# Windowed attention by halves of the rows, beside a mixture of experts: moving the first half's output groups among the second half's rounds

## The chip, the core and the metric

The kernel runs on one core of a Trainium2 chip. The core has five engines with instruction queues of their own: TensorE (PE) multiplies matrices, VectorE (DVE) does elementwise work and reductions, ScalarE (ACT) evaluates functions, GpSimd (POOL) does slower elementwise work and issues indirect DMAs, and SyncE (SP) issues DMAs. Each engine works through its queue in order and waits on semaphores for the others. The metric is the device time of one execution in microseconds (us); a run is repeated and its median is given.

## What is computed

One transformer block on x of shape 2 x 1024 x 256. The rows are normalized; windowed attention and a routed mixture of experts both read the normalized rows, and their results are added to x:

```
xn = layernorm(x)
x  = x + attn(xn) + ffn(xn)
# attn: tok = xn as tokens of 16 values; q, k, v = tok @ qkv_w
#   per branch (8 of the 16 channels): windows of 8 tokens, along a line or down a column
#   out = softmax(q * scale @ k^T) @ v + conv3x3(v) + bias
#   att = concat(out1, out2) @ proj_w + proj_b
#   tok + (att - mean) * rsqrt(var + eps) * ln_w + ln_b, transposed back to rows
# ffn: scores = sigmoid(xn @ gate^T); 6 of 16 experts a row, from 2 of 4 groups
#   out = sum over experts of weight * (silu(xn @ g^T) * (xn @ u^T)) @ d^T
#   + a shared expert of twice the width
```

All values are 32-bit floats.

## The kernel before

After the layer norm, the routing and the shared expert (the first 110 us or so), the kernel is one loop over 55 units of routed expert work with two half units each (the loop over `u` at L1098). A unit is either "six" (two of the six most wanted experts of one of 16 sorted tiles of 128 rows, `xsT`) or "extra" (two lists of 128 rows that have another expert, gathered by an indirect DMA, `gathered`, L978, and turned on TensorE, `turned`, L984). For one half unit TensorE multiplies rows by the expert's two input matrices into `pr_u` (`up`, L849), ScalarE takes Silu into `sg`, and VectorE multiplies `sg`, the row's weight and the second product into `hms` (L856). A unit later TensorE transposes `hms` into `ph` (`hidden`, L863), ScalarE copies it to `hT`, and another unit later the down product goes into `pr_y` (L879, L887), is copied to `ysum` and is added to the output in memory by an indirect DMA from GpSimd's queue (`to_out`, L992, its DMA at L994). All writes that add to the output go one after another, since each waits for the landing of the one before.

Attention is done beside this loop. It is written as a list of small steps, a generator `walk` (`attention_steps`, L1052), each with an estimated cost on VectorE and on TensorE. After each half unit the loop takes steps as long as VectorE's sum of costs is not ahead of `pace` times TensorE's (L1120). `pace` is made so that the walk is done when `END` = 72 us of TensorE's work is still left (L1074 to L1078). The order in which instructions stand in each engine's queue then comes from a scheduler in the framework, which may move an instruction ahead of others that are not ready in its reckoning.

The walk has four rounds, `attention(b, h)` for two images b and two halves h of a row's 256 values (h is 128 columns). A round (L653 to L745) gathers its input from the transposed rows `xnT`, projects it on TensorE in eight matmuls `pq` whose results ScalarE copies to `qk` and `v`, and then works on VectorE: four products `pr` and four reductions `s` (scores), a maximum, the subtraction, Exp on ScalarE, four products `pv` and four reductions `o`, a division into `xo`. TensorE turns `xo` (`po`, L725) and ScalarE copies it into `oT` (L727), one tile of 4 groups x 2 halves x 4 x 128 columns. The rounds go b by b: (0,0), (0,1), (1,0), (1,1).

After the fourth round come eight output groups, `attended(g, h, ...)` for g = 0 to 3 and both halves (L761): four matmuls of 512 columns into `pp` (three for the convolution, from `xnT`, one for the projection of `oT`; the first and the last group read a shifted copy of the edge rows, `xe`, made by `edges`, L747), a bias on ScalarE into `a` (L780), four transposes `pa`, Square (L787), a sum on VectorE (`var`, L789), Sqrt on ScalarE (L790), a reciprocal (L791), a product (L792), and on GpSimd a multiplication by `lw` (L793) and two additions of the normalized row `xr` into `att` (L798). `xr` is loaded for each g by a DMA from GpSimd's queue (L769). After g = 1 and g = 3, four DMAs of 256 KB each add `att` to the output (`attention_added`, L1065, L1068). The working tiles `a`, `sq` and `xr` use the three buffers `f1024` that the rounds had, so no group can start before the last round is over. ScalarE has one table of functions loaded at a time: Sqrt, Exp and Silu are in different ones, and a change shows as ACT_TABLE_LOAD.

While the loop runs, the lists of the extra units are made (`lists_begun`, L900) in `room_`, a part of `ysum`, until half unit 45.

Of the kernel before, what the change touches and what calls it, by code (L numbers as in the profile page):

```python
# [8 lines left out]
F32 = mybir.dt.float32  # L9
# [3 lines left out]
AF = mybir.ActivationFunctionType  # L13
# [9 lines left out]
P = 128  # L23
B, H, W = 2, 1024, 256
# [27 lines left out]
def csw_block_moe(ctx: ExitStack, tc: tile.TileContext, x, qkv_w, conv_w0, conv_b0, conv_w1, conv_b1,  # L52
# [33 lines left out]
    def by_hl(t):  # L86
        return t.rearrange("(p l) d -> p l d", l=16)
# [659 lines left out]
    def edges():  # L747

        xe = [work.tile([P, 2, 4, P], F32, tag=tag, name="xe") for tag in ("v", "xo")]
        for t in xe:
            nc.gpsimd.memset(t, 0.0)
        pairs = xnT.rearrange("p h l (q e) -> p l h q e", e=2)
        for h in range(2):
            above, below = (t[:, h].rearrange("p l (q e) -> p l q e", e=2) for t in xe)
            nc.vector.tensor_copy(above[:, :, :, 1], pairs[:, 12:16, h, :, 0])
            nc.vector.tensor_copy(below[:, :, :, 0], pairs[:, 0:4, h, :, 1])
        return xe

    def attended(g, h, xe, att):  # L761

        if not last_room:
            last_room.extend(work.tile([P, 2, TB], F32, tag="f1024", name=name, bufs=3) for name in ("xr", "a", "sq"))
        xr = last_room[0].rearrange("p l (k d) -> p (l k) d", d=W)
        quarters = [t[:, n] for t in last_room[1:] for n in range(2)]
        a_, sq_ = quarters[(2 * g + h) % 3], quarters[3]
        if h == 0:
            nc.gpsimd.dma_start(out=xr, in_=by_hl(xw_d[0:ROWS, :])[:, 4 * g : 4 * g + 4, 0:W])  # L769
# [3 lines left out]
                 (lp[:, 1], xnT[:, h, 4 * g - 4 : 4 * g, :] if g > 0 else xe[0][:, h]),  # L773
                 (lp[:, 2], xnT[:, h, 4 * g + 4 : 4 * g + 8, :] if g < 3 else xe[1][:, h]),
# [4 lines left out]
        aT = a_.rearrange("p (l q) -> p l q", l=4)  # L779
        nc.scalar.activation(aT, pp, AF.Identity, bias=pbc)  # L780
# [5 lines left out]
        sq, a = (t.rearrange("p (n c) -> p n c", c=C) for t in (sq_, a_))  # L786
# [6 lines left out]
        nc.gpsimd.tensor_tensor(a, a, lw.unsqueeze(1).to_broadcast(wide), ALU.mult)  # L793
        for m in range(2):
            to = att[m].rearrange("p n (l d) -> p n l d", d=16)[:, :, 4 * g : 4 * g + 4, 8 * h : 8 * h + 8]
            one = a.rearrange("p (l t) c -> p c l t", t=8)[:, 8 * m : 8 * m + 8]
            two = xr.rearrange("p l (t c) -> p c l t", c=C)[:, 8 * m : 8 * m + 8, :, 8 * h : 8 * h + 8]
            nc.gpsimd.tensor_tensor(to, one, two, ALU.add)  # L798

    last_room = []  # L800
# [97 lines left out]
    listed = []  # L898

    def lists_begun():  # L900
# [47 lines left out]
        lists_ended()  # L948
        yield
# [102 lines left out]
    def attention_steps():  # L1052
        for b in range(B):
            for h in range(2):
                yield from attention(b, h)
        xe = []
        yield 0.6, 0.0, lambda: xe.extend(edges())
        att.extend(work.tile([P, 8, W], F32, tag=tag, name="att") for tag in ("prod", "qk"))
        for g in range(4):
            for h in range(2):  # L1060
                yield 1.4, 3.9, lambda: attended(g, h, xe, att)
            if g % 2:
                waiting.extend([lambda m=m, b=b, n=g // 2: attention_added(m, b, n) for m in range(2) for b in range(B)])

# [9 lines left out]
    END = 72  # L1074
    in_walk = [8 * 1.0 + 4 * (16 * 2.3 + 3.3 + 2.5 + 1.5 + 1.4) + 0.6 + 8 * 1.4, 8 * 0.1 + 4 * 6.2 + 8 * 3.9]
# [22 lines left out]
    for u in range(len(laid_out) + 2):  # L1098
        for q in range(2):
# [20 lines left out]
            while step and done[0] <= pace * done[1]:  # L1120
# [82 lines left out]
```

## Time and profile before

| | |
|---|---|
| runs | 447.02, 447.40, 449.18 us, median 447.4 |
| profiled execution | 447.97 us, span from first to last instruction 446.3 us |
| busy: PE, DVE, ACT, POOL | 393.4, 291.5, 214.1, 197.9 us |
| mean granted TensorE clock | 0.987 |
| four rounds of attention, on VectorE | 4 x 4 of each of pr, s, pv, o at 2.27 to 2.29 us |
| output groups on TensorE | 347.5 to 397.7 us from the start of the span |

Durations and positions are those of one profiled execution. The busy time of an engine is that in which an instruction of it runs; "waited for" is idle time before an instruction with the instruction that ended it. Matmuls overlap, and the profile shows each as longer than its share of a dense sequence, so I take TensorE's costs from the chain that ended last, where successive pieces don't overlap. In the loop, a half unit's product pr_u takes TensorE 1.28 us.

### The profile page before, as it was taken

What the parts mean: (1) busy time and instruction counts of PE and PEld (TensorE: products, weight loads), DVE (VectorE), ACT (ScalarE), POOL (GpSimd) and SP (SyncE); (2) the same over time, 40 slices, a digit from 0 to 9 for tenths busy, and PEclk for the clock granted to TensorE, in tenths of its full rate; (3) what the DMA queues carried; (4) which work ended last, traced back from release to release, by engine and by line L of the source; (5) the groups of instructions that cost most, each with busy time, mean ns of one, the idle gap of its engine ahead of it and who ended that gap; (6) DMA issues with size and microseconds to landing.
All of it is one profiled execution on the core that took longest, in us unless ns stands there. A gap on an engine that the chain in (4) does not pass through costs nothing.

```text
span 446.3 us, 6293 instructions
## 1 busy us (share of the span) xinstructions
PE 393.4 (88%) x1668; PEld 246.3 (55%) x1669; DVE 291.5 (65%) x515; ACT 214.1 (48%) x535; POOL 197.9 (44%) x207
## 2 busy tenths in 40 slices
PE   0999999997899788998897999999998899979990
PEld 0435465664466555565564666656665555446670
DVE  4624958635699979289995999959999223322210
ACT  2945258322544442643635456364533657774320
POOL 7300000314273299457524245615554274779432
PEclk9999999999999999999999999999999999998997
DMA  8999941324023101101212124210332101822922
GB/s 232 338 304 321 275 154 30 64 67 86 25 71 73 32 25 34 29 23 33 38 39 60 35 43 81 47 36 24 69 90 56 22 14 57 103 68 74 126 44 24
DMA packets 40178, 37.56 MB, mean 84 GB/s; under 512 B 5300, under 2 KB 37616, under 8 KB 40112
## 3 DMA queue, kind: packets, MB, share of 16 engines
q0 software_dynamic: 11616, 13.52, 18.4%
q1 hardware_dynamic: 27472, 22.59, 16.4%
q10 hardware_dynamic: 1056, 1.05, 0.7%
q8 instruction: 15, 0.25, 0.2%
q14 instruction: 19, 0.16, 0.1%
HBM read 27.70 MB, written 12.45 MB: 90 GB/s over the span
## 4 chain that ended last, share of the span: by engine, by line
DVE 38%; PE 30%; DMA 10%; issue 8%; ACT 7%; POOL 5%; DVEq 0%; POOLq 0%; ACTq 0%; SPq 0%
DVE s L688 6%; PE pr_u L853 6%; DVE pv L705 6%; DVE pr L684 5%; DVE o L710 5%; DVE hms L856 5%; PE pp L777 4%; PE pq L671 3%; PE pr_y L879 3%; DMA out_dram<-ysum,lists 3%; PE pg L273 3%; PE py L288 2%; DMA xg<-xw_d,lists 2%; PE pu L273 2%; DMA xx<-in_x_dram 2%
## 5 line engine op out<-in xcount | busy, mean ns | idle before, releaser
L853 PE MATMUL pr_u<-w1s,xsT 128*128 x384 | 128.4, 468 | 3.4 <-DVE hms L856 2.4
L853 PEld LDWEIGHTS pr_u<-w1s,xsT 128*128 128x128 f32 x384 | 69.9, 191 | 39.4 <-issue 7.7
L994 POOL DMA_INDIRECT out_dram<-ysum,lists x30 | 57.2, 1908 | 77.4 <-ACT ysum L1040 20.3
L855 ACT ACTIVATE sg<-pr_u 128x176 f32<-128x176 f32 x110 | 34.7, 317 | 77.1 <-PE pr_u L853 70.2
L856 DVE SCALAR_TENSOR_TENSOR hms<-sg,w,pr_u 128x176 f32<-128x176 f32 x96 | 36.8, 387 | 35.5 <-ACT sg L855 35.5
L684 DVE TENSOR_TENSOR pr<-qk 128x2048 f32<-128x2048 f32 x16 | 36.6, 2288 | 17.6 <-ACT qk L673 17.2
L705 DVE TENSOR_TENSOR pv<-s,v 128x2048 f32<-128x2048 f32 x16 | 36.5, 2284 | 2.5 <-ACT s L696 2.4
L867 PE MATMUL ph<-ident,hms 128*128 128x128 f32 x165 | 31.7, 282 | 5.5 <-DVE hms L856 2.9
L688 DVE TENSOR_REDUCE s<-pr 128x256 f32<-128x2048 f32 x16 | 36.5, 2279 | 0.1
L955 POOL TENSOR_SCALAR ysum<-row_h,spot 128x128 f16<-128x128 f16 x26 | 28.0, 1094 | 19.2 <-PE rows_of L946 14.9
L710 DVE TENSOR_REDUCE o<-pv 128x256 f32<-128x2048 f32 x16 | 36.3, 2269 | 0.0
L980 POOL DMA_INDIRECT xg<-xw_d,lists x14 | 21.6, 1540 | 29.3 <-DVE hms L856 15.5
L867 PEld LDWEIGHTS ph<-ident,hms 128*128 128x128 f32 x165 | 21.5, 144 | 23.2 <-DVE hms L856 6.9
L291 POOL DMA_DIRECT2D out_dram<-ysh x4 | 3.7, 928 | 64.5 <-ACT ysh L289 64.5
L817 POOL DMA_INDIRECT xg<-xw_d,lists x16 | 19.8, 1239 | 25.4 <-PE ph L867 9.3
L879 PE MATMUL pr_y<-w2a,hT 128*128 x96 | 29.1, 386 | 0.0
L879 PE MATMUL pr_y<-wts,hT 128*128 128x256 f32 x96 | 29.0, 384 | 0.0
L879 PE MATMUL pr_y<-w2b,hT 112*128 x96 | 28.8, 381 | 0.0
L671 PE MATMUL pq<-wq,rows 128*128 128x384 f32 x64 | 25.1, 506 | 3.3 <-ACT oT L727 1.9
L869 ACT COPY hT<-ph 128x384 f32<-128x384 f32 x55 | 26.4, 480 | 2.8 <-PE ph L867 1.8
L853 PE MATMUL pr_u<-w1s,xd 128*128 x56 | 20.4, 487 | 6.6 <-ACT xd L989 6.6
L288 PE MATMUL py<-room 128*128 128x256 f32 x96 | 23.9, 387 | 0.7 <-DVE room L282 0.7
(403 smaller groups left out, 712.2 us busy)
## 6 DMA issues: line engine op xcount, KB each, us to landing
w1s<-in_w_dram SPq DMA_DIRECT2D x22, 256.0 KB, 4.4
wts<-in_w_dram SPq DMA_DIRECT2D x55, 64.0 KB, 2.1
wts<-in_w_dram SPq DMA_DIRECT2D x55, 48.0 KB, 1.7
xw_d<-xx SPq DMA_DIRECT2D x4, 544.0 KB, 4.6
w2a<-in_w_dram SPq DMA_DIRECT2D x4, 512.0 KB, 9.4
out_dram<-ysh POOLq DMA_DIRECT2D x4, 512.0 KB, 5.6
xr<-xw_d POOLq DMA_DIRECT2D x4, 512.0 KB, 5.0
out_dram<-att POOLq DMA_DIRECT2D x8, 256.0 KB, 6.4
```

What stands on the lines that cost most here:

```text
L288: nc.tensor.matmul(py, lhsT=hms[k, m][:, P * c : P * c + P], rhs=w2h[:, m], start=(m == 0), stop=(m == 2))
L671: nc.tensor.matmul(pq.rearrange("p s t c -> p (s t c)"), lhsT=rows[:, i], rhs=wq.rearrange("p s t c -> p (s t c)"), start=True, stop=True)
L684: nc.vector.tensor_tensor(pr, q_.unsqueeze(3).to_broadcast(full), k_.unsqueeze(2).to_broadcast(full), ALU.mult)
L688: nc.vector.tensor_reduce(out=s[:, n : n + NW], in_=held.pop(n), axis=AX.X, op=ALU.add)
L705: nc.vector.tensor_tensor(pr, s[:, n : n + NW].unsqueeze(3).to_broadcast(full), v[:, br, m : m + NW].unsqueeze(2).to_broadcast(full), ALU. ...
L710: nc.vector.tensor_reduce(out=o[:, n : n + NW], in_=held.pop(n), axis=AX.X, op=ALU.add)
L853: nc.tensor.matmul(pu, lhsT=lhs[:, h, :], rhs=w1s[:, :, h, bass.ds(e * I, I)], start=(h == 0), stop=(h == 1))
L855: nc.scalar.activation(sg, pu[:, 0, :], AF.Silu)
L856: nc.vector.scalar_tensor_tensor(hm[:, 0:I], sg, w, pu[:, 1, :], op0=ALU.mult, op1=ALU.mult)
L867: nc.tensor.transpose(ph[:, s, :], units[:, P * s : P * s + P], ident)
L879: nc.tensor.matmul(py, lhsT=l_, rhs=r_, start=start and n == 0, stop=stop and n == 2)
L994: nc.gpsimd.indirect_dma_start(out=out_rows, out_offset=bass.IndirectOffsetOnAxis(ap=index, axis=0), in_=ys, in_offset=None, bounds_check= ...
```

## The change

The rounds are ordered by half: (0,0), (1,0), (0,1), (1,1). After two rounds `oT` is complete for half 0, so its output groups can start. `attended` is cut into two steps: `attended` (the four matmuls and the bias) and `normed` (the transposes, the norm and the multiplication by `lw`). The eight steps of half 0 are put among the rounds of half 1, one ahead of every fourth step of a round from its second VectorE step on. The bias result and the normalized values are written back into `oT`, in the place of the group's input, so no working tile is needed but one for the squares; this and the edge rows lie in `room_`, and a step of 3 us or more of TensorE work waits until the lists are made (`made`). The edge copy is made for one half and one edge at a time, four times, in one tile. The additions of `xr` (`added`) stay behind the last round for both halves, since `att` uses the rounds' buffers; the loads of `xr` for three groups are issued together there, the fourth behind the additions of group 0. `END` goes from 72 to 50, and the cost of the steps is counted anew.

```diff
--- before.py
+++ after.py
@@ -744,46 +744,41 @@
             steps.append((0.3, 0.5, lambda i=i: transposed(i)))
         return steps
-    def edges():
-        xe = [work.tile([P, 2, 4, P], F32, tag=tag, name="xe") for tag in ("v", "xo")]
-        for t in xe:
-            nc.gpsimd.memset(t, 0.0)
-        pairs = xnT.rearrange("p h l (q e) -> p l h q e", e=2)
-        for h in range(2):
-            above, below = (t[:, h].rearrange("p l (q e) -> p l q e", e=2) for t in xe)
-            nc.vector.tensor_copy(above[:, :, :, 1], pairs[:, 12:16, h, :, 0])
-            nc.vector.tensor_copy(below[:, :, :, 0], pairs[:, 0:4, h, :, 1])
-        return xe
-    def attended(g, h, xe, att):
-        if not last_room:
-            last_room.extend(work.tile([P, 2, TB], F32, tag="f1024", name=name, bufs=3) for name in ("xr", "a", "sq"))
-        xr = last_room[0].rearrange("p l (k d) -> p (l k) d", d=W)
-        quarters = [t[:, n] for t in last_room[1:] for n in range(2)]
-        a_, sq_ = quarters[(2 * g + h) % 3], quarters[3]
-        if h == 0:
-            nc.gpsimd.dma_start(out=xr, in_=by_hl(xw_d[0:ROWS, :])[:, 4 * g : 4 * g + 4, 0:W])
+    def edge(h, n):
+        t = room_[:, TB : 2 * TB].rearrange("p (l q) -> p l q", l=4)
+        nc.gpsimd.memset(t, 0.0)
+        pairs = xnT[:, h].rearrange("p l (q e) -> p l q e", e=2)
+        nc.vector.tensor_copy(t.rearrange("p l (q e) -> p l q e", e=2)[:, :, :, 1 - n],
+                              pairs[:, 0:4, :, 1] if n else pairs[:, 12:16, :, 0])
+        return t
+    def attended(g, h):
+        xe = edge(h, g // 3) if g % 3 == 0 else None
         pp = ps_m.tile([P, 4, P], F32, tag="m", name="pp")
         terms = [(lp[:, 0], xnT[:, h, 4 * g : 4 * g + 4, :]),
-                 (lp[:, 1], xnT[:, h, 4 * g - 4 : 4 * g, :] if g > 0 else xe[0][:, h]),
-                 (lp[:, 2], xnT[:, h, 4 * g + 4 : 4 * g + 8, :] if g < 3 else xe[1][:, h]),
+                 (lp[:, 1], xnT[:, h, 4 * g - 4 : 4 * g, :] if g > 0 else xe),
+                 (lp[:, 2], xnT[:, h, 4 * g + 4 : 4 * g + 8, :] if g < 3 else xe),
                  (wp, oT[:, g, h])]
         for n, (l_, r_) in enumerate(terms):
             nc.tensor.matmul(pp.rearrange("p l q -> p (l q)"), lhsT=l_.rearrange("p t c -> p (t c)"),
                              rhs=r_.rearrange("p l q -> p (l q)"), start=(n == 0), stop=(n == len(terms) - 1))
-        aT = a_.rearrange("p (l q) -> p l q", l=4)
-        nc.scalar.activation(aT, pp, AF.Identity, bias=pbc)
+        nc.scalar.activation(oT[:, g, h], pp, AF.Identity, bias=pbc)
+    def normed(g, h):
+        aT = oT[:, g, h]
         pa = ps_m.tile([P, 4, P], F32, tag="m", name="pa")
         for l in range(4):
             nc.tensor.transpose(pa[:, l, :], aT[:, l, :], ident)
         rows_a = pa.rearrange("p l (t c) -> p (l t) c", c=C)
         wide = [P, 32, C]
-        sq, a = (t.rearrange("p (n c) -> p n c", c=C) for t in (sq_, a_))
+        sq, a = room_[:, 0:TB].rearrange("p (n c) -> p n c", c=C), aT.rearrange("p l (t c) -> p (l t) c", c=C)
         nc.scalar.activation(sq, rows_a, AF.Square)
         var = small.tile([P, 32], F32, tag="var", name="var")
         nc.vector.tensor_reduce(out=var, in_=sq, axis=AX.X, op=ALU.add)
@@ -791,13 +786,19 @@
         nc.vector.reciprocal(var, var)
         nc.vector.tensor_tensor(a, rows_a, var.unsqueeze(2).to_broadcast(wide), ALU.mult)
         nc.gpsimd.tensor_tensor(a, a, lw.unsqueeze(1).to_broadcast(wide), ALU.mult)
+    def rows_of_x(g):
+        xr = work.tile([P, 2, TB], F32, tag="f1024", name="xr", bufs=3).rearrange("p l (k d) -> p (l k) d", d=W)
+        nc.gpsimd.dma_start(out=xr, in_=by_hl(xw_d[0:ROWS, :])[:, 4 * g : 4 * g + 4, 0:W])
+        return xr
+    def added(g, h, xr, att):
+        a = oT[:, g, h].rearrange("p l (t c) -> p (l t) c", c=C)
         for m in range(2):
             to = att[m].rearrange("p n (l d) -> p n l d", d=16)[:, :, 4 * g : 4 * g + 4, 8 * h : 8 * h + 8]
             one = a.rearrange("p (l t) c -> p c l t", t=8)[:, 8 * m : 8 * m + 8]
             two = xr.rearrange("p l (t c) -> p c l t", c=C)[:, 8 * m : 8 * m + 8, :, 8 * h : 8 * h + 8]
             nc.gpsimd.tensor_tensor(to, one, two, ALU.add)
-    last_room = []
     xsT = big.tile([P, NTL, 2, P], F32, name="xsT", tag="xx")
@@ -895,7 +896,7 @@
     at_ = room_[:, 0 : 3 * 257].rearrange("p (a n) -> p a n", a=3)
     begin = room_[:, 800:832].rearrange("p (a e) -> p a e", a=2)
     ends = route.tile([P, E], F32, name="ends")
-    listed = []
+    listed, made = [], []
     def lists_begun():
         flagged = room_[:, 832:960].bitcast(BF16)
@@ -946,6 +947,7 @@
                 nc.tensor.matmul(listed[0], lhsT=spot[:, 0:P], rhs=spot[:, P:], start=(n == 2), stop=(n == NX + 1))
             yield
         lists_ended()
+        made.append(True)
         yield
     def pair_listed(n):
@@ -1050,17 +1052,29 @@
         yield from attention_steps()
     def attention_steps():
-        for b in range(B):
-            for h in range(2):
-                yield from attention(b, h)
-        xe = []
-        yield 0.6, 0.0, lambda: xe.extend(edges())
+        ahead_ = [step for g in range(4) for step in of_group(g, 0)]
+        for h in range(2):
+            for b in range(B):
+                for n, step in enumerate(attention(b, h)):
+                    if h == 1 and n >= 10 and n % 4 == 2 and ahead_:
+                        yield ahead_.pop(0)
+                    yield step
+        yield from ahead_
+        xr = [rows_of_x(g) for g in range(3)]
         att.extend(work.tile([P, 8, W], F32, tag=tag, name="att") for tag in ("prod", "qk"))
         for g in range(4):
-            for h in range(2):
-                yield 1.4, 3.9, lambda: attended(g, h, xe, att)
+            yield 0.0, 0.0, lambda: added(g, 0, xr[g], att)
+            yield from of_group(g, 1)
+            yield 0.0, 0.0, lambda: added(g, 1, xr[g], att)
+            if g == 0:
+                yield 0.0, 0.0, lambda: xr.append(rows_of_x(3))
             if g % 2:
                 waiting.extend([lambda m=m, b=b, n=g // 2: attention_added(m, b, n) for m in range(2) for b in range(B)])
+    def of_group(g, h):
+        yield 0.2, 3.45, lambda: attended(g, h)
+        yield 1.4, 0.45, lambda: normed(g, h)
     def attention_added(m, b, n):
@@ -1071,8 +1085,8 @@
     of_slot = {"six": (0.5, 2.0), "extra": (0.8, 2.5)}
     of_tile = (0.75, 0.25)
-    END = 72
-    in_walk = [8 * 1.0 + 4 * (16 * 2.3 + 3.3 + 2.5 + 1.5 + 1.4) + 0.6 + 8 * 1.4, 8 * 0.1 + 4 * 6.2 + 8 * 3.9]
+    END = 50
+    in_walk = [8 * 1.0 + 4 * (16 * 2.3 + 3.3 + 2.5 + 1.5 + 1.4) + 8 * 1.6, 8 * 0.1 + 4 * 6.2 + 8 * 3.9]
     done = [0.0, 0.0]
     whole = [in_walk[n] + NTL * TOPK * of_slot["six"][n] + NL * of_slot["extra"][n] + NTL * of_tile[n] for n in range(2)]
     pace = (whole[0] - END * of_slot["six"][0] / of_slot["six"][1]) / (whole[1] - END)
@@ -1117,7 +1131,7 @@
                 if 0 <= u - 2 < len(laid_out):
                     finished(laid_out[u - 2], hT_.pop(u - 2), wts[:, (u - 2) % 3], begun_.pop(u - 2))
             counted(of_slot[laid_out[min(u, len(laid_out) - 1)][0]])
-            while step and done[0] <= pace * done[1]:
+            while step and done[0] <= pace * done[1] and (made or step[1] < 3):
                 step[2]()
                 counted(step)
                 last, step = step, next(walk, None)
```

## The prediction

> **What bounds the kernel now.** I read the shares by engine first (TensorE 88% busy, VectorE 65%), then busy time by stretch, since a mean hides stages. The stretches are the three last attention rounds (from the first product to the last division) and the stretch of the eight output groups.
>
> ```profile
> core 0: us, PE busy (x) PEld busy (x) DVE busy (x) ACT busy (x) POOL busy (x), PEclk, DMA share, GB/s
> ...
> 188.00:238.50 50.50, 45.26 (x193) 30.02 (x191) 48.10 (x47) 21.61 (x68) 26.86 (x28) 1.00 0.16 36
> ...
> 244.30:292.00 47.70, 45.30 (x188) 30.26 (x186) 46.71 (x41) 22.83 (x65) 22.15 (x12) 1.00 0.27 53
> ...
> 298.00:346.00 48.00, 44.65 (x188) 29.54 (x187) 46.98 (x43) 20.91 (x63) 23.15 (x13) 1.00 0.26 56
> 346.00:400.00 54.00, 50.55 (x180) 27.56 (x177) 16.43 (x33) 37.26 (x55) 32.07 (x29) 1.00 0.31 53
> ```
>
> Columns are stretch, length, then PE, PE loads, DVE, ACT, POOL busy. In the rounds VectorE is busy 141.8 of 146.2 us (97%): it is the limit, and TensorE (135.2 of 146.2) follows it. In the last row it is the reverse: VectorE 16.4 of 54, TensorE 50.6 of 54. So 16 us of dense TensorE work stands where VectorE is free, beside rounds where VectorE is full. What TensorE waits for from 188 to 346 us (total, times, longest):
>
> ```profile
> PE pr_u L853 <- ACT xd L989: 4.1, 10, 0.5
> PE po L725 <- DVE xo L718: 3.2, 3, 1.6
> PE ph L867 <- DVE hms L856: 2.0, 5, 0.6
> PE pq L671 <- ACT oT L727: 1.2, 2, 0.7
> PE ph L867 <- ACT hT L869: 1.1, 1, 1.1
> ```
>
> 6.3 us (po for xo, ph for hms and hT) are lateness of VectorE and of the activations behind it. The other 5.9 (xd, oT, a gather of 0.6) are single round trips that no order removes. Then the chain that ended last, at the start of the output groups:
>
> ```profile
> 345.68 0.67 PE po L725 x4
> ...
> 347.48 3.71 PE pp L777 x8
> 351.22 0.70 ACT a L780
> 351.96 0.66 PE pa L783 x4
> ...
> 355.01 3.45 PE pp L777 x8
> ```
>
> The first group starts at 347.5, when the last round's oT is there. One costs TensorE 3.45 us (pp, eight passes) and 0.67 (pa). Last the GpSimd queue to the end:
>
> ```profile
> 381.22 4.82 POOL L1068 DMA_DIRECT2D out_dram<-att  x4
> ...
> 392.52 1.67 POOL L994 DMA_INDIRECT out_dram<-ysum,lists  x1 [4.37 <-DMA out_dram<-att]
> ...
> 411.38 4.77 POOL L1068 DMA_DIRECT2D out_dram<-att  x4
> 421.95 1.66 POOL L994 DMA_INDIRECT out_dram<-ysum,lists  x1 [5.80 <-DMA out_dram<-att]
> ...
> 439.04 1.55 POOL L994 DMA_INDIRECT out_dram<-ysum,lists  x1 [3.06 <-DMA out_dram<-ysum,lists]
> ```
>
> The end is not TensorE's: its last matmul is over at 435.9. After the second block of four att stores (411.38) come five scatters, each waiting for the landing before it (10.6 us for the stores, then 17.1 from first to last scatter), and 7.3 us more to 446.3. From that block to the end is 34.9 us, and it is a chain of GpSimd and DMA.
>
> **The change part by part.** Sums are made against the profiled execution: span 446.3, time 447.97, so 1.67 lies around it; the median of the runs, 447.4, is 0.6 lower, which I take off at the end.
>
> *Order.* The order of the built program shows that the four groups of half 0 now stand among the two rounds of half 1, one at each of the half units 53, 61, 70 and 75 of 114, and that the last group stands just before the last pair of extra units, as before. The wait for finished lists (made) holds nothing: they are done at half unit 45. The rounds end 4 half units later (91, not 87).
>
> *Moved TensorE work.* Ahead of the last stretch now lie 4 groups of 3.45 + 0.67 = 16.5 us and 4 half units of experts: 4 x 1.28 (pr_u) + 2 x (0.33 + 1.30) (ph, pr_y) + 0.6 (px) + 0.8 (waits for xd) = 9.8. The start of the last stretch moves from 347.5 to 373.8. TensorE's sum is unchanged: this alone is worth nothing.
>
> *Relief of VectorE.* From 188 to 346 it worked 142.7 of 158 us (90%, gaps between the rounds counted). It gets four norms (var 0.69, reciprocal 0.35, product 0.69: 6.9), edge copies (0.6) and 4 more hms (0.39 each: 1.6), 151.8 in all, over 158 + 26.3: 82%. Inside the rounds, whose three gaps of 5.3 us for projections stay, it is 152 of 168 or 90% instead of 97%. Of the 6.3 us of lateness I take half, -3.2 (ends 0 and -6.3): a hms must still stand behind a 2.29 us product, but no more behind several. The rounds of half 0 are paced 7% slower (pace falls from 1.18 to 1.10); of 4.7 us of such waits from 117 to 188 I take -1.0 (0 to -2). Groups 0 to 3 now have half units of experts between pp and pa, where pa waited 2.3 us for a in 346 to 400: half of it, -1.2.
>
> *Activations in the rounds.* A norm brings sq 0.60, a table load, sqrt 0.32, and a load back to Silu:
>
> ```profile
> 353.53 1.28 ACT L790 ACT_TABLE_LOAD   x1
> 354.82 0.32 ACT L790 ACTIVATE var<-var,eps 128x32 f32<-128x32 f32 x1
> 355.16 1.28 ACT L855 ACT_TABLE_LOAD   x1
> ```
>
> Loads in total fall from 30 to 29; four pairs move into the rounds, in front of sg and hT. The Trainium skill (ScalarE: Activation LUTs, "What ACT_TABLE_LOAD costs") gives a switch of set 1283 ns and a drain of 1380, 2.66 us together. The row has the 1283, and sqrt starts 0.01 us after its load ends: no drain lies between. By the page a norm would hold ScalarE 5.3 us in loads, by the row 2.6. The nearest row for what TensorE loses is the Exp of the three rounds, also two loads around one activation: at 214 ph waits 1.15 + 0.31, at 267 nothing, at 323 0.31. Mean 0.6, so four norms cost +2.4 (0 to +6; by the page about double). Below nothing is excluded, since no load is taken away here.
>
> *GpSimd in the rounds.* Multiplying by lw (1.27 us alone) now runs beside 2.29 us products that read two SBUF operands. The Trainium skill (SBUF, State Buffer, "Who interferes with whom") speaks against that: such an instruction and a GpSimd instruction that reads SBUF shut each other out, whichever starts first. The trace has GpSimd's side: a spots comparison takes 0.59 alone and 2.62 at 161.70, beside pv (161.55 to 163.85). By the rule VectorE could lose 1.27 x 4 = 5.1 as well; in the rows pv takes 2.30 where GpSimd began 0.3 earlier and 2.28 elsewhere. I take 0 for VectorE, and up to 2.3 x 4 on GpSimd, which is idle half of the rounds (26.9 of 50.5 busy); without that cover the queue's gathers would be 2 us late, where the one issued at 251.86 has its px at 262.19, 10 us later. The four memsets replace two of twice the size; each is issued when the edge before it has been read, far ahead of its group, so pp doesn't wait for them: 0 (up to +1).
>
> *The last stretch.* From its start T the groups of half 1 take 4 x (3.45 + 1.28 + 0.67) + 2 x 1.65 = 24.9 us. GpSimd: its six additions of half 0 whose xr is there (1.05 each) and three xr issues are over by about T+1; memset to T+2.5; then the first lw product waits for group 0's norm until T+9.3 (as at 356.48, 9.0 after pp), additions to T+12.7, the fourth xr is issued behind them and lands 4.3 us later, additions of group 3 to T+19.6, lw and additions of group 1 to T+23. First block of stores at T+23; the scatter behind it waits for their landing, 11.3 us as at 392.52: T+34.3. One lw product and two additions follow: second block at T+39.2, end at T+39.2+34.9 = T+74.1. Before it was 446.3 - 347.5 = 98.8. So this stretch is 24.7 shorter where 26.3 moved ahead of it: +1.6 (-1 to +5, if xr lands late or the first additions reach past T+2.5). If the queue is faster than that, TensorE is late next, over at T+58 and worth T+68.
>
> *Sum.* 446.3 - 3.2 - 1.0 - 1.2 + 2.4 + 1.6 = 444.9; + 1.67 = 446.6 against 447.97; on the runs' median 446.0. (About 0.5% is what a measurement here can tell from no change: 445.2 to 449.6.)
>
> **The rivals.**
> *Faster: VectorE was the whole limit.* For it: 97% in three rounds. Against it: TensorE waited for it only 6.3 us there. All 6.3 go, the loads find cover: 446.0 - 3.1 - 2.4 = 440.5.
> *Slower: VectorE waits inside its rounds for the norms.* It works in order; a norm makes it wait for sq and for sqrt. In the output groups of before it waited 14.9 us for sq (7 times) and 9.9 for sqrt (8 times), 3.4 a group, free there because it had nothing else. In a round that is 90% full, 4 x 3.4 = 13.5 is paid, less the 7 us of slack gained: +6.5, 452.5. It decides where the two waits exceed about 1.7 us a norm. Against it: the built order puts a product or a reduction between var and reciprocal of each group. The last queue, at its worse end, gives +3.4 more on the likeliest and lies in the same class.
> *It doesn't do what it says* (the groups stay at the end): excluded by the built order.
>
> **How the numbers follow.** About 446.0: 0.37; its own bounds are 442 to 451. Faster, near 440.5: 0.31. Slower, near 452.5 or by the queue: 0.32. The range goes from 441 to 453.5. Faster by over 0.5%: 0.31, within: 0.37, slower: 0.32.
>
> **What would show it.** Right: in the rounds of half 1 VectorE near 90%, po without a wait for xo, last stretch about 74 us from its first pp, VectorE waiting under 1 us a norm for sq and sqrt. Relief wrong: ph's waits for hms and hT as before. Activation cost wrong: ph's waits for hT over 4 us. Queue wrong: second block of stores more than 41 us after the first pp of half 1. All wrong if TensorE's clock, 0.99 here, were lower.

## The result, and the profile after

The changed kernel takes 460.84 us (median of 4 runs, 459.69 to 462.64), beside 447.75 for the kernel before on the same chip: ratio 1.0276, 95% interval 1.0231 to 1.0321. It is slower, by 13 us. The profiled execution took 460.98 us, with a span of 459.3 and a mean granted TensorE clock of 0.962 (0.987 before).

The same stretches as before, that is the three last rounds, each from its first product to its last division, and then the last stretch cut at its two store blocks:

```profile
core 0: us, PE busy (x) PEld busy (x) DVE busy (x) ACT busy (x) POOL busy (x), PEclk, DMA share, GB/s
195.00:250.20 55.20, 46.98 (x192) 31.32 (x191) 48.75 (x48) 20.99 (x65) 28.33 (x25) 0.94 0.19 39
260.40:312.00 51.60, 48.63 (x188) 30.50 (x187) 49.77 (x46) 28.39 (x69) 20.86 (x12) 1.00 0.21 40
321.20:372.60 51.40, 46.05 (x180) 29.77 (x178) 49.84 (x45) 25.77 (x67) 21.75 (x14) 0.93 0.23 48
381.60:407.60 26.00, 24.94 (x87) 13.64 (x88) 7.39 (x15) 17.40 (x28) 17.98 (x17) 1.00 0.24 61
407.60:424.10 16.50, 16.27 (x70) 11.23 (x70) 4.42 (x11) 8.39 (x19) 13.31 (x11) 1.00 0.73 95
424.10:459.30 35.20, 15.56 (x69) 11.58 (x68) 2.38 (x6) 4.57 (x12) 12.60 (x10) 0.79 0.44 55
```

VectorE is as full as before in the two rounds that took the norms (96% and 97%), and the clock is below 1 in two of the three rounds. In the last row no engine is half busy: the kernel waits there for transfers. TensorE's waits from 195 to 380 us, beside those shown of before (total, times, longest):

```profile
PE pr_u L854 <- ACT xd L991: 8.1, 9, 4.4
PE px__2443 L989 <- DMA xg<-xw_d,lists: 2.3, 1, 2.3
PE px__2461 L989 <- DMA xg<-xw_d,lists: 2.2, 1, 2.2
PE pr_u L854 <- DVE hms L857: 1.9, 3, 1.2
PE ph L868 <- ACT hT L870: 1.6, 2, 1.1
```

The waits of po for xo are gone. In their place stand a wait of 4.4 us for one copy xd, and two for the gathers of the first extra unit. From 117 to 195 us there are two more that the kernel before doesn't have at this length:

```profile
PE rows_of L947 <- POOL ysum L958: 2.6, 1, 2.6
PE px__1371 L822 <- DMA xg<-xw_d,lists: 1.5, 1, 1.5
```

GpSimd's queue to the end:

```profile
401.89 2.15 POOL L801 TENSOR_TENSOR att<-oT,xr 128x256 f32<-128x256 f32 x2 [1.55 <-DMA xr<-xw_d]
...
407.63 4.84 POOL L1082 DMA_DIRECT2D out_dram<-att  x4 [0.17 <-POOL att L801]
...
418.98 1.66 POOL L996 DMA_INDIRECT out_dram<-ysum,lists  x1 [3.01 <-DMA out_dram<-att]
420.06 1.88 POOL L788 TENSOR_TENSOR oT<-oT,lw 128x512 f32<-128x512 f32 x1
422.02 2.14 POOL L801 TENSOR_TENSOR att<-oT,xr 128x256 f32<-128x256 f32 x2
424.10 4.75 POOL L1082 DMA_DIRECT2D out_dram<-att  x4
435.05 1.65 POOL L996 DMA_INDIRECT out_dram<-ysum,lists  x1 [6.21 <-ACT sg L856]
439.73 1.57 POOL L996 DMA_INDIRECT out_dram<-ysum,lists  x1 [3.03 <-DMA out_dram<-ysum,lists]
...
452.20 1.53 POOL L996 DMA_INDIRECT out_dram<-ysum,lists  x1 [2.96 <-DMA out_dram<-ysum,lists]
```

From the second store block to the end it is 35.2 us (34.9 before), with the same five scatters behind it. So the whole loss lies ahead of that block: it stands at 424.1 instead of 411.4. TensorE is no longer near the end: its last matmul is over at 439.7, 19.6 us before it (435.9 and 10.4 before).

### The profile page after: what moved, and what is told of

It is laid out like the page before. It is cut to its first block, busy times and chain, and to the rows that moved or that the text cites. A ratio compares the mean times of both kernels' runs of the same rounds, so it can differ in the third digit from the quotient of the medians.

```text
span 459.3 us, 6285 instructions
## 1 busy us (share of the span) xinstructions
PE 397.2 (86%) x1668; PEld 249.1 (54%) x1669; DVE 292.9 (64%) x515; ACT 213.2 (46%) x534; POOL 194.2 (42%) x209
## 4 chain that ended last, share of the span: by engine, by line
PE 42%; DVE 18%; DMA 14%; issue 10%; POOL 8%; ACT 6%; DVEq 0%; POOLq 0%; SPq 0%; ACTq 0%
PE pr_u L854 13%; PE pr_y L880 5%; PE pq L671 5%; DMA xg<-xw_d,lists 5%; PE pp L770 4%; DMA out_dram<-att 4%; DMA out_dram<-ysum,lists 3%; PE pg L273 3%; DVE pv L705 2%; PE py L288 2%; DVE pr L684 2%; DVE o L710 2%; PE pu L273 2%; DVE s L688 2%; DVE hms L857 2%
## 5 line engine op out<-in xcount | busy, mean ns | idle before, releaser
L854 PE MATMUL pr_u<-w1s,xsT 128*128 x384 | 130.6, 473 | 2.9 <-DVE hms L857 2.6
L996 POOL DMA_INDIRECT out_dram<-ysum,lists x30 | 52.4, 1746 | 90.1 <-ACT ysum L1035 39.2
L982 POOL DMA_INDIRECT xg<-xw_d,lists x14 | 24.5, 1750 | 22.4 <-DVE hms L857 20.0
L868 PE MATMUL ph<-ident,hms 128*128 128x128 f32 x165 | 29.3, 281 | 3.1 <-ACT hT L870 1.6
L957 POOL TENSOR_SCALAR ysum<-row_h,spot 128x128 f16<-128x128 f16 x26 | 22.7, 885 | 21.2 <-PE rows_of L947 10.0
L818 POOL DMA_INDIRECT xg<-xw_d,lists x16 | 19.7, 1233 | 27.2 <-PE px__1202 L822 9.3
L854 PE MATMUL pr_u<-w1s,xd 128*128 x56 | 23.1, 540 | 9.2 <-ACT xd L991 9.1
L671 PE MATMUL pq<-wq,rows 128*128 128x384 f32 x64 | 25.5, 510 | 2.6 <-ACT oT L727 1.4
```

The lines of the kernel that those rows point to most:

```text
L671: nc.tensor.matmul(pq.rearrange("p s t c -> p (s t c)"), lhsT=rows[:, i], rhs=wq.rearrange("p s t c -> p (s t c)"), start=True, stop=True)
L854: nc.tensor.matmul(pu, lhsT=lhs[:, h, :], rhs=w1s[:, :, h, bass.ds(e * I, I)], start=(h == 0), stop=(h == 1))
L868: nc.tensor.transpose(ph[:, s, :], units[:, P * s : P * s + P], ident)
L996: nc.gpsimd.indirect_dma_start(out=out_rows, out_offset=bass.IndirectOffsetOnAxis(ap=index, axis=0), in_=ys, in_offset=None, bounds_check= ...
```

## The experiments

Two numbers follow each run through what follows: T, the first pp behind the last round, and the second store block. All times are medians, with the ratio to the kernel before measured beside them (448.8 to 450.0 there, 447.75 for the changed kernel). Where the text says "less" or "worth" without a ratio, it compares the medians, which is good to some 2 us. Behind T stand the last four groups in the changed kernel and its versions, but all eight in the kernel before, the b_ runs, a_late and a_late62.

Positions are from one profiled execution of each kernel, whose own time can lie some us beside the median (a_place64: 466.25). Such executions differ before any edit comes into play: the 217th matmul pr_u, ahead of the first moved group, starts at 258.0 us in the changed kernel, at 256.1 in a_nosqrt and at 255.5 in a_place and a_late. I call what an execution is ahead there its lead at 258 us.

| run | us | ratio, 95% | T | 2nd store block | scatters behind | block to end | TensorE's end |
|---|---|---|---|---|---|---|---|
| before | 447.75 | | 347.5 | 411.4 | 5 | 34.9 | 435.9 |
| changed | 460.84 | 1.0276 (1.0231, 1.0321) | 381.6 | 424.1 | 5 | 35.2 | 439.7 |
| a_vadds | 457.38 | 1.0210 (1.0146, 1.0274) | 383.6 | 420.1 | 5 | 34.8 | 445.4 |
| a_nosqrt | 455.36 | 1.0145 (1.0095, 1.0195) | 376.4 | 416.3 | 5 | 35.5 | 433.3 |
| a_end72 | 459.06 | 1.0223 (1.0171, 1.0276) | 361.2 | 403.1 | 9 | 53.8 | 448.8 |
| a_late | 454.91 | 1.0130 (1.0082, 1.0178) | 371.9 | 430.9 | 2 | 22.1 | 430.8 |
| b_end50 | 461.75 | 1.0247 (1.0191, 1.0303) | 375.3 | 438.0 | 2 | 22.6 | 436.5 |
| b_order | 449.53 | 0.9979 (0.9946, 1.0013) | 346.8 | 412.6 | 5 | 35.7 | 436.9 |
| a_place | 455.37 | 1.0121 (1.0068, 1.0173) | 375.9 | 416.4 | 5 | 35.7 | 433.9 |
| a_xrsp | 460.72 | 1.0233 (1.0178, 1.0288) | 381.5 | 419.7 | 5 | 39.5 | 438.9 |
| a_nostore2 | 452.54 | 1.0045 (1.0023, 1.0067) | 380.4 | none | | | 438.8 |
| b_nostore2 | 448.04 | 0.9972 (0.9948, 0.9996) | 346.7 | none | | | 433.6 |
| a_place58 | 460.67 | 1.0228 (1.0185, 1.0272) | 371.4 | 415.0 | 7 | 44.5 | 442.3 |
| a_place64 | 461.98 | 1.0246 (1.0208, 1.0283) | 374.1 | 416.0 | 8 | 48.5 | 449.1 |
| a_late62 | 458.83 | 1.0175 (1.0134, 1.0216) | 362.2 | 428.1 | 4 | 30.4 | 435.5 |
| a_lists | 459.93 | 1.0224 (1.0172, 1.0275) | 380.7 | 422.8 | 5 | 35.3 | 438.7 |
| a_place_lists | 455.81 | 1.0172 (1.0123, 1.0221) | 375.1 | 416.9 | 5 | 35.4 | 432.6 |
| a_place_lists_sp | 457.33 | 1.0174 (1.0123, 1.0225) | 376.6 | 416.5 | 5 | 39.5 | 434.1 |

The column "block to end" is nearly a function of the scatters behind the block: 11 us until the first of them, 4.4 for each further one, 7 behind the last. With 2, 5, 7 and 9 scatters this gives 22.4, 35.6, 44.4 and 53.2; measured 22.1, 35.2, 44.5 and 53.8. The three figures were taken from these runs, so this is a fit and no forecast. It holds for both kernels. Each scatter waits for the landing of the one before, as the 3.03 and 2.96 us of idle in the queue show.

**Is the end GpSimd's chain?** Two edits ask it: the additions on another engine, and the second store block left out.

```diff
-            nc.gpsimd.tensor_tensor(to, one, two, ALU.add)
+            nc.vector.tensor_tensor(to, one, two, ALU.add)
```

> The changed kernel, with the sixteen additions of the attention's rows to x (line 801) on VectorE instead of GpSimd. Theory 1 (GpSimd's chain sets the end): in the last stretch GpSimd works through 4 x (2.1 us of additions of half 0 + 1.3 of lw + 2.1 of additions of half 1) = 22 us, 11 us of scatters and 9.6 us of stores, 43 us, and the second store block comes at T + 42.5; with the additions gone, it has 26 us, the second block comes 9 us earlier or more, the last matmul to end falls from 20 us to about 10.5 as in the kernel before, and the time from 461 to about 452. Theory 2 (TensorE's waits and clock in the rounds, not GpSimd): the last scatters are spaced by their own landing whatever the store does, and the time stays at 460 to 461.

Measured: 457.38. The way from T to the store block is 6.0 us shorter (36.5 instead of 42.5), but T is 2.0 later, so the block came 4 us earlier, not 9. VectorE, which has to wait for rows of x and for the product with lw, now holds up the hms behind these additions (waits from 380 to 445 us):

```profile
PE ph L868 <- DVE hms L857: 4.5, 3, 3.1
PE pr_u L854 <- ACT xd L991: 1.9, 2, 1.1
PE pa L778 <- DVE oT L787: 1.5, 1, 1.5
```

TensorE's end went to 445.4, 9.4 us before the end. So theory 1 fits in kind and missed in size, as the relieved queue bought a new wait. The time alone could not tell: its interval overlaps that of the changed kernel.

```diff
-            if g % 2:
+            if g == 1:
```

> The changed kernel without its second store block: columns 128 to 255 of the attention's share of out are left out, all else is done. Theory of two bounds (the end is the later of TensorE's last matmul + 8 to 10 us, and the second store block + 35 us): TensorE's last matmul stays at 439 to 440, the scatters run as their data come, and the time falls to 448 to 451. Rival (the scatters' own landings, about 4.5 us each, set the end whatever the store does): 458 to 461.

Measured: 452.54, 8.3 less, from TensorE's unchanged 438.8 by 11.2 us to the end. Here the scatters run as their data come:

```profile
422.82 1.58 POOL L996 DMA_INDIRECT out_dram<-ysum,lists  x1 [0.15 <-issue]
427.51 1.55 POOL L996 DMA_INDIRECT out_dram<-ysum,lists  x1 [3.10 <-ACT hT L870]
431.98 1.55 POOL L996 DMA_INDIRECT out_dram<-ysum,lists  x1 [2.92 <-DMA out_dram<-ysum,lists]
435.44 1.55 POOL L996 DMA_INDIRECT out_dram<-ysum,lists  x1 [1.90 <-ACT hT L870]
440.02 1.55 POOL L996 DMA_INDIRECT out_dram<-ysum,lists  x1 [3.03 <-ACTq L1152]
```

The last stands at 440.0 instead of 452.2, though it is 10.0 us from there to the end instead of 7.1. So the second store block, with what waits for it, costs the changed kernel some 8 us. The same edit on the kernel before tells whether this is the change's own.

> The kernel before without its second store block: columns 128 to 255 of the attention's share of out are left out. Theory of two bounds: TensorE's last matmul at 436 is only 10.4 us from the end there, so little is to be had: 443 to 448. If the kernel before hung on GpSimd's chain as much as the changed one (which fell by 8.3 us): 437 to 441.

Measured: 448.04, ratio 0.9972, so some 1.5 us less. The last scatter stands at 434.3, directly behind TensorE's end, instead of 439.0; but here too the way from it to the end is 3 us longer (10.2 instead of 7.2), which takes back most of the 4.7 us. So most of the 8 us are the changed kernel's own.

**What in the rounds makes the block late?** First the square root:

```diff
-        nc.scalar.activation(var, var, AF.Sqrt, bias=eps, scale=1.0 / C)
+        nc.scalar.activation(var, var, AF.Identity, bias=eps, scale=1.0 / C)
```

> The changed kernel with Identity in place of Sqrt in the eight norms (line 785): the square root is left out, and with it the table loads around it. Theory 1 (the norms' table loads in the rounds cost TensorE's wait for xd of 4.37 us at 346 and, behind it, some 3.4 us of matmuls at half clock): the wait is gone, TensorE's last matmul ends 4 to 8 us earlier. As the end hangs on GpSimd's chain behind TensorE, the time falls by about the same, to 453 to 457. Theory 2 (the wait is the Exp block's own, as in the kernel before): the time stays within 1.5 us of 461.

Measured: 455.36. T is 5.2 us earlier, TensorE's end 6.3. Of both, 1.8 us are the lead at 258 us, which the edit can't have made. Behind it TensorE gains 1.3 us at the first two norms in the rounds and 2.0 at the fourth. What stood at the fourth is seen on ScalarE in the changed kernel:

```profile
343.37 0.60 ACT L782 ACTIVATE ysum<-pa 128x512 f32<-128x512 f32 x1
343.99 1.28 ACT L696 ACT_TABLE_LOAD   x1
345.72 1.06 ACT L696 ACTIVATE s<-s 128x1024 f32<-128x1024 f32 x1 [0.45 <-DVE s L695]
346.80 1.28 ACT L785 ACT_TABLE_LOAD   x1
348.09 0.32 ACT L785 ACTIVATE var<-var,eps 128x32 f32<-128x32 f32 x1
348.43 1.28 ACT L856 ACT_TABLE_LOAD   x1
349.73 0.32 ACT L856 ACTIVATE sg<-pr_u 128x176 f32<-128x176 f32 x1
349.94 0.47 ACT L870 COPY hT<-ph 128x384 f32<-128x384 f32 x1
350.30 0.39 ACT L991 COPY xd<-px__3417 128x256 f32<-128x256 f32 x1
```

The fourth norm stands ahead of step 18 of its round, directly behind the Exp. Three loads of 1.28 us, Exp and Sqrt are in ScalarE's queue ahead of a copy xd that TensorE has needed since 346.4. Moving the norm two steps on (and with it the projection at the same step of the round before) keeps the norms' loads, 30 in all instead of 29, and takes the collision away:

```diff
-                    if h == 1 and n >= 10 and n % 4 == 2 and ahead_:
+                    if h == 1 and n in (10, 14, 20, 22, 26) and ahead_:
```

> The changed kernel with the pieces of half 0 put in ahead of steps 10, 14, 20, 22 and 26 of a round instead of 10, 14, 18, 22 and 26, so that the fourth norm's Sqrt no longer stands beside the round's Exp on ScalarE; its table loads stay. Theory 1 (the collision of Exp's, Sqrt's and Silu's table loads ahead of the xd copy at 346 costs the 4.4 us wait and some 3.4 us of half clock): TensorE's last matmul ends at 432 to 435 instead of 439.7, and the time is 452 to 456, as without the square root. Theory 2 (the loads cost wherever they stand): 459 to 462.

Measured: 455.37, the same as without any square root, and clear of the changed kernel (the intervals don't overlap). This is TensorE's wait at that place in the changed kernel, without the square root and with the norm moved:

```profile
350.74 2.71 PE L854 MATMUL pr_u<-w1s,xd 128*128 x4 [4.37 <-ACT xd L991]
346.49 1.78 PE L854 MATMUL pr_u<-w1s,xd 128*128 x4 [3.29 <-ACT xd L991]
345.51 0.33 PE L868 MATMUL ph<-ident,hms 128*128 128x128 f32 x1 [2.46 <-ACT hT L870]
```

Most of the wait is that of the Exp and its own two loads, and stays. From 341.6 to 357.6 us of the changed kernel, TensorE gains 2.0 us without the square root and 2.4 with the norm moved; both are 3.3 us ahead at the end of this stretch, leads at 258 us (1.8 and 2.5) taken off. So the place of the one norm explains most of what the square root costs ahead of T, and the other loads cost nothing that these runs can tell. How much of the 5.5 us between the medians is the collision they can't tell either, as single executions are 2 us apart ahead of it.

Next the work itself, left behind the last round with all else as changed:

```diff
-                    if h == 1 and n >= 10 and n % 4 == 2 and ahead_:
-                        yield ahead_.pop(0)
```

> The changed kernel without the change's core: half 0's projections and norms wait until the last round is done, as half 1's do; order of the rounds, pace, tiles and the separate additions stay as changed. Theory 1 (the moved norms cost, by table loads and their waits in the rounds): the rounds run as before, the time returns to 447 to 451. Theory 2 (order of the rounds, pace and GpSimd's chain cost): with eight groups behind a slower pace the end is even later, 462 to 470.

Measured: 454.91, between the two theories. Beside a_place it says that moving the groups, once they are well placed, is worth nothing either way that can be told (454.9 and 455.4). Some 6 us of loss then stay with the pace, the order and the separate additions. The order alone and the pace alone, in the kernel before:

```diff
-        for b in range(B):
-            for h in range(2):
+        for h in range(2):
+            for b in range(B):
                 yield from attention(b, h)
```

> The kernel before with its four rounds in the order of the halves, (0,0), (1,0), (0,1), (1,1), and nothing else. The rounds are alike and all four lie ahead of the first group, so every theory held now says no change: 446 to 450. If it is over 452, part of the loss belongs to the order itself.

```diff
-    END = 72
+    END = 50
```

> The kernel before with END 50 in place of 72 and nothing else: the slower pace alone. Theory of two bounds (the end is the later of TensorE's last matmul + 10 us and the second store block + some 35 us, as GpSimd's queue lets each store and scatter land before the next): TensorE gains as in the run with late groups (its last matmul near 430), but the groups and so the second store block come 10 to 19 us later than 411, and the time is 452 to 458. Theory that the pace costs nothing or helps: 443 to 448.

Measured: 449.53 and 461.75. The order costs nothing. The pace alone costs the kernel before about 12 us: TensorE's end stays (436.5), but T is 27.8 us later, and the eight groups with GpSimd's chain behind it. This run also has the long waits of the changed kernel for the lists and their gathers (rows_of 2.7 and px 5.8 us, where the kernel before has 0.6 and 0.9), and the same long gaps between the rounds, from the last division to the next first product: 14.6, 10.2 and 10.9 us (changed 14.6, 10.2 and 9.2; before 9.0, 5.7 and 5.9). Both come with the pace. In the changed kernel the old pace was no way back:

> The changed kernel with END 72 as before: the steps of the rounds come earlier among the units. Theory 1 (the slower pace makes the lists and so the first gathers late against the units, rows_of 2.6 us and px 4.5 us of TensorE's waits, with half clock behind them): these waits shrink to the 1.2 us of the kernel before, and the time falls by 4 to 7 us, to 454 to 457. Theory 2 (the pace only shifts where TensorE works, the end is GpSimd's chain): the last groups come some 8 units earlier, GpSimd's chain with them, and the last matmul to end falls from 20 to 10.5 us while TensorE's end stays at 440, so 450 to 452. Theory 3 (the pace was slowed because VectorE can't follow): waits for VectorE come in, 461 or more.

Measured: 459.06. T is 20 us earlier and the store block 21, but nine scatters now stand behind the block instead of five, and their count gives 53.2 of the 53.8 us from it to the end. TensorE now waits for VectorE, from 195 to 360 us:

```profile
PE po L725 <- DVE xo L718: 6.4, 3, 3.0
PE ph L868 <- ACT hT L870: 4.5, 2, 3.4
PE ph L868 <- DVE hms L857: 2.6, 4, 1.0
```

It ends at 448.8, just ahead of the last scatter (449.5), so the scatters' chain and TensorE end together here. Paces in between, with the norms well placed or with the groups late:

> The changed kernel with the pieces of half 0 away from Exp (steps 10, 14, 20, 22, 26) and END 58 instead of 50. By the order as built, the last groups go out four half units earlier (87 to 91 instead of 91 to 95), some 8 to 10 us. Theory of two bounds: the second store block comes at 406 to 409 instead of 416, TensorE's last matmul at 434 to 439 as VectorE comes nearer to the units, and the time is 445 to 450, the first version of the change that is no slower than the kernel before. Rival (slack on GpSimd is used up by more scatters behind the store, 4.5 us each): 452 to 456.

> As the run before, with END 64. Theory of two bounds: the store block comes some 15 us earlier than with 50, now TensorE is the bound: waits for xo and the lists' gathers return as with END 72 (TensorE's end 448.8 there), so 447 to 453, a minimum lying at 56 to 62. Rival: 444 or less, the gain goes on with END.

> The changed kernel with half 0's groups behind the last round, as half 1's, and END 62 instead of 50: the last groups go out at half units 91 to 99 instead of 97 to 105. Theory of two bounds: second store block 12 us earlier than 430.9, TensorE's last matmul at 431 to 435, time 444 to 449. Rival (moving the norms into the rounds is worth something by itself): at or above the run with END 58 and moved norms by 2 us or more.

Measured: 460.67, 461.98 and 458.83, all worse than their likes with END 50 (455.37, 454.91). The rival of a_place58 was right in its mechanism, and the loss was larger than it said: the block hardly moved (416.4 with END 50, then 415.0 and 416.0), while two and three more scatters of 4.4 us went behind it. That VectorE, with four norms more to do, holds the block there is my reading, and no run shows it. The profiled execution of a_place64 is also its slowest. None of the paces tried between 50 and 72 is better than 50.

**Transfers.** The rows of x from SP's queue, and the lists made earlier:

```diff
-        nc.gpsimd.dma_start(out=xr, in_=by_hl(xw_d[0:ROWS, :])[:, 4 * g : 4 * g + 4, 0:W])
+        nc.sync.dma_start(out=xr, in_=by_hl(xw_d[0:ROWS, :])[:, 4 * g : 4 * g + 4, 0:W])
```

> The changed kernel with the four loads of x's rows for the additions (line 792) issued from SP's queue instead of GpSimd's. Theory 1 (GpSimd's chain sets the end, and 7.4 us of it in the last stretch are waits for these rows): the waits shrink, the second store block comes 3 to 7 us earlier than 424, and the time is 454 to 458. Rival (the loads wait on SP for a free buffer and hold up the units' weights behind them): TensorE waits for wts, 461 or more.

Measured: 460.72. The block did come 4.4 us earlier, as expected, but the end gave it back: the first scatter 1 us later behind the block, and 10.2 us instead of 7.1 from the last scatter to the end. The same 3 us stand in a_place_lists_sp, a_nostore2 and b_nostore2 (10.0 to 10.2 us from the last scatter to the end) and in no other run (6.9 to 7.4). These four have in common that GpSimd's queue issues four transfers fewer. What the 3 us are the trace doesn't show.

```diff
                 next(extras_ if i < 14 else lists_, None)
+            if i in (20, 26, 32, 38):
+                next(lists_, None)
```

> The changed kernel with four of the list steps taken at half units 20, 26, 32 and 38 in addition, so that the lists are ready four half units earlier and the first extra unit's gathers can start in time. Theory 1 (the late gathers at 234 to 240 cost T 4.5 us of wait and some 2 us of half clock): these waits go to 1 us or less, the second store block comes at 417 to 419 instead of 424, with five scatters behind, and the time is 453 to 456. Theory 2 (VectorE is full in these rounds, so what TensorE gains it waits for elsewhere): 459 to 461.

> Both mends in one: the norms away from Exp (steps 10, 14, 20, 22, 26) and the lists four half units earlier. Theory 1 (the two add up): second store block at 409 to 412, the forecast's 410, and with five scatters behind it a time of 446 to 449, that of the kernel before. Theory 2 (they share one slack): 453 to 456, as with the places alone.

> As the run before, with the loads of x's rows on SP's queue too. If the waits for these rows on GpSimd (7.4 us in the last stretch) still set its chain: 2 to 4 us less than without, 443 to 447, the best version and below the kernel before. If, as in the run with that edit alone, the chain takes the gain back behind the store: the same within 1 us.

Measured: 459.93, 455.81 and 457.33. In a_lists these two waits for the gathers are gone, and this stands in the list of waits from 195 to 380 us instead:

```profile
PE pr_u L854 <- ACT xd L991: 8.6, 10, 4.4
PE ph L868 <- DVE hms L857: 3.0, 1, 3.0
```

T moved by 0.9 us. That is what theory 2 said: in a round that VectorE fills, TensorE waits for VectorE where it doesn't wait for the gather. No version of the changed kernel that I tried beats the kernel before.

## Why the prediction was wrong, point by point

The forecast was 446.0 and a span of 444.9; the span is 459.3, 14.4 more. The failed step is the start of the last stretch, T: "from 347.5 to 373.8" less the gains plus the loads, so 370.8. It came at 381.6, 10.8 late. The other 3.6 are in the last stretch. Within T the sum let only the waits move that it named. It held "the other 5.9 (xd, oT, a gather of 0.6)" for round trips that stay, had nothing for a wait on the lists, and took the clock as 0.99. From 117 us to the last po these waits grew: for gathers from 0.9 to 6.4 us, for the lists (rows_of) from 0.6 to 2.6, for xd from 4.1 to 8.1. That is some 11.5 us, more than the named ones gave back, and the clock fell behind them.

- *Order and moved TensorE work: right.* T without gains was put at 373.8. TensorE's busy time ahead of po grew by 30.4 us, from 309.0 to 339.4; 25.5 were forecast (26.3 less 0.8 of waits). The other 4.9 are covered by the lower clock: busy time times the missing share of the clock, summed over slices of 2 us, gives an estimate of 8.1 us lost ahead of po, and of 1.6 in the kernel before. That the move "alone is worth nothing" is what a_late against a_place shows.
- *Relief of VectorE, -5.4: its own waits fell, TensorE's idle time didn't.* The waits of po went from 3.2 to 0, those of ph and pr_u for hms and hT from 7.9 to 5.6, and pa's from 2.3 to 0.3. But TensorE's idle time ahead of po rose, from 36.8 to 40.4, by the waits above. The reason given, a load of 90% in the rounds, did not come true: VectorE is at 96 to 97% in those that took the norms. It stood idle in longer gaps instead, 30.3 us in three gaps where it was 18.8, and b_end50 has the same gaps with no group moved. An edit that took a wait away there (a_lists) found the next one.
- *"Paced slower", -1.0: right for its own waits, and blind to others.* Those fell from 4.7 to 1.7 us ahead of the second round. But b_end50 shows that the pace alone brings some 7 of the 11.5 us above. That the rounds end later among the units was in the sum, in its 373.8; the 12 us that b_end50 loses are this with all eight groups still behind, and no measure of this term.
- *Activations, +2.4 (0 to +6): near in size, wrong in picture.* Ahead of T, TensorE gains 3.3 us behind the 258 us in a_nosqrt and in a_place. But the cost is not alike for four norms: most of it lies at the fourth, which stood behind an Exp, and I had not looked at which step each piece precedes. The announced sign, waits of ph for hT over 4 us, did not come (1.6): it was xd that waited.
- *Clock: listed as what would make all wrong, and it happened.* Behind the 4.4 us of idle at 346.4 the matmuls ran at half clock:

```profile
core 0: us, PE busy (x) PEld busy (x) DVE busy (x) ACT busy (x) POOL busy (x), PEclk, DMA share, GB/s
238.00:242.00 4.00, 2.47 (x5) 1.43 (x6) 1.29 (x1) 0.00 (x0) 0.89 (x1) 0.50 0.28 70
...
348.00:352.00 4.00, 1.26 (x2) 0.84 (x3) 4.00 (x6) 2.65 (x6) 0.88 (x1) 0.65 0.18 30
352.00:356.00 4.00, 4.00 (x12) 2.89 (x11) 4.00 (x4) 1.17 (x3) 2.28 (x3) 0.50 0.43 130
356.00:360.00 4.00, 4.00 (x16) 2.67 (x15) 3.53 (x4) 0.64 (x2) 3.78 (x3) 1.00 0.23 64
```

  Four matmuls pr_u took 2.71 us at 350.7, instead of 1.45. The Trainium skill (TensorE: Matmul & The Clock Gate, "What's actually happening") says that an idle window of about 3.4 us halves the clock, and a busy one of that length gives it back. The rows at 348 to 360 agree that a wait longer than this halves it; the clock was back at 356, after 5.3 us of work. Shorter waits than the page's were enough too. At 238 the clock was halved behind two of 2.3 and 2.2 us with 0.7 us of transposes between. In a_place it fell behind the one wait of 2.46 us, and only when work had begun again: it was 1.00 from 345 to 346 us, 0.72 in the next and 0.50 in the two behind that.
- *GpSimd and VectorE beside each other, 0: not contradicted.* The mean product pv went from 2.28 to 2.33 us. I did not try it apart.
- *The last stretch, +1.6 (-1 to +5): T+77.7 instead of T+74.1, 3.6 more.* The first block stood at T+26.0 (forecast T+23), the second at T+42.5 (T+39.2), the end 35.2 behind it (34.9). So the sign announced for a wrong queue, a second block behind T+41, came. The 3.3 us are waits for rows of x (3.64, 2.21 and 1.55 us on GpSimd), where I had taken three loads as landed by T+1; with the loads on SP the block stands at T+38.2.
- *The sum.* Of the 10.8 us of T, 4.9 are TensorE's busy time beyond the forecast, and 5.8 its idle time: 3.6 more than before, where the sum had 2.2 less.
- *The rivals.* None came by its mechanism. For sq or the square root VectorE never waited in the rounds of half 1, as the order said. The last queue at its worse end, +3.4 in the slower rival's last sentence, is about what the last stretch cost; the larger part of the loss lies ahead of T.

What stays open: the 3 us behind the last scatter when GpSimd's queue issues four transfers fewer; whether the gathers and the norm's place together would have brought T to the forecast, as a_place_lists came to 375.1 with a lead of its own; and why the changed kernel with late groups (454.9) is 7 us better than the kernel before at the same END (461.8). Of these, 3.4 are an earlier T, but TensorE was 2.8 us ahead already at 119 us (the 25th pr_u at 117.1 and 119.9), where the first round's products begin; 3.7 are a shorter way from T to the second block (59.0 us instead of 62.7).

## What to carry to other kernels

Find the chain that ends last, and ask of every edit when it lets that chain's first link start; a pace that eases two busy engines can delay a third that sets the end. A sum in which only the named waits move leaves out those that the change makes longer. Slack read as a mean over rounds and gaps may all lie in the gaps. Where pieces with table loads are put among others, look at each piece's neighbours: moving one norm away from an Exp brought as much as leaving out the square root of all eight. Before two profiled executions are compared, see whether they agree ahead of the edit.

## What the hardware showed that I had not expected

- A stall of TensorE goes on costing when it is over, as the clock falls with it: behind 4.4 us of idle some 2.6 us were lost to half clock in the changed kernel (an estimate from the busy time and the granted clock at 350 to 356 us), behind 3.3 and 2.5 us in a_nosqrt and a_place 1.6 and 1.7.
- A further scatter with addition in a queue costs 4.4 us, though its issue takes 1.55: the next one waits for it to land. The count of scatters left behind the last store fits the rest of the span within 1 us in 11 of 13 executions that had such a block in the changed kernel or its versions; the two others had the loads on SP.
- An addition of two strided 128x256 tiles takes VectorE 0.61 us (a_vadds) and GpSimd 1.10 (changed), in the median.
